# A graph layer on one core: spares' slots by one shifted row, two running extremes in bf16, places loaded one by one

## The chip, the cores and the metric

The kernel runs on one core of a Trainium2 chip. The metric is the device time of one execution in microseconds (us). The core's engines run side by side and wait for each other through semaphores: TensorE (PE, with its weight loads as PEld), VectorE (DVE), ScalarE (ACT), GpSimd (POOL) and SyncE (SP). A q behind a name (DVEq) is the engine's sequencer, which hands the instructions on in their order and does register work itself.

## The reference

400,000 edges, sorted by their destination, join 12,500 nodes of 128 features. Each edge carries the row of its source, through one of two weight matrices by the edge's type; the messages of a destination are summed; a self product, relu, a residual and a layer norm follow.

```python
msg = jnp.where((edge_types == 0)[:, None], Xs @ W_data.T + b_data, Xs @ W_control.T + b_control)
agg = jax.ops.segment_sum(msg, dst, num_segments=X.shape[0])
out = jax.nn.relu(agg + (X @ W_self.T + b_self))
x = _layernorm(x + out, axis=-1)
```

The kernel sums source rows for each destination and type first and multiplies by the weights once for each destination.

## The kernel before

Rows of x are split into three bf16 parts whose sum is the fp32 value; a row is 3 x 128 numbers. The edges come in 25 groups (`NG`) of 125 chunks of 128 edges. A group's chunks are cut into windows: "p" chunks fetch their rows from DRAM by an indirect DMA of GpSimd (985 of them, `fetch`), "e" chunks, 20 to a set, take them out of SBUF by products with 0/1 matrices on TensorE (`pick` in `picked`, L929). There are 107 sets, numbered `w`, and each is prepared two or three turns ahead.

**A set's slots.** Each of the 128 lanes holds 20 edges of a set; an edge gets a cell (which block of x its source lies in) and a rank in that cell (`block_matrix`, `ranks`, `rank_matrix`, `put`). A cell has room for 32 edges. Those of a higher rank are spares: at most `TOP` = 7 in a lane and at most `OVF` = 64 in a set. Spares of two sets, an even one and the next odd one, are placed together, so this happens 54 times (53 pairs and one set alone): `over` finds each lane's spares and packs them as `bits`; `over_before` has TensorE count the spares of the lanes before (`both["before"]`, one column for each set, in PSUM); `over_matrix` (L558) has DVE compare a table with that count; `turn` (L562) has TensorE multiply the 0/1 result with the bits; `keep` (L573 to L579) has ACT copy the outcome out and make row numbers of it, from which GpSimd fetches the spares' rows (L904).

The table `slot_col` (L368) holds o - j for spare j and slot o, 7 x 64 numbers, and the result `om_all` is 7 x 2 x 64, so that each of 7 products has the slots of both sets as its 128 columns, and 6 columns of bits stream through.

**Ranges.** `prep(g)` (L473) turns a group's edges into codes: `rel` is the destination relative to the window's start, for p and for e. Four instructions (L499) keep, in fp32, the running maximum and minimum of `rel` less its bound. At the end `check_all` makes one flag of these and other checks, and a long path would run if it were set.

**Places.** Each window's sums are added to the group's rows of sums at a place that depends on the data. `place_of` (L802) loads a group's ten places into DVE registers by one instruction, at the group's first use (25 loads), and the range check on the chip is skipped because the values were limited before. `accumulate` (L813) forms the address in the sequencer and adds (232 adds of sums `acc` and 125 of counts `cnt`).

The program order comes from `merged`, which sorts units by hand-written positions inside a turn, and from a scheduler that orders each engine's instructions.

Of the kernel before, what the change touches and what calls it, by code (L numbers as in the profile page):

```python
# [8 lines left out]
FP = mybir.dt.float32  # L9
# [10 lines left out]
P = 128  # L20
# [186 lines left out]
def short_path(ctx, tc, const, ident, eps, wT, brow, bad, x, src, dst, etype, ws, bs, out):  # L207
# [156 lines left out]
    blks = [keep.tile([P, NE, 2 * EC], BF, name=f"blk{k}") for k in range(3)]  # L364
    for t in blks:
        nc.vector.memset(t, -1.0)
    slot_col = keep.tile([P, TOP, OVF], BF, name="slot_col")
    nc.vector.tensor_copy(slot_col, iota([TOP, OVF], [[-1, TOP], [1, OVF]], 0, 0, "i5"))  # L368

    om_all = [keep.tile([P, TOP, 2, OVF], BF, name=f"om_all{k}") for k in range(2)]  # L370
    for t in om_all:
        nc.vector.memset(t, 0.0)

# [9 lines left out]
    nc.vector.memset(one_col, 0.0)  # L383
    nc.vector.memset(one_col[:, 0:PARTS], 1.0)

    worst = keep.tile([P, 5, P], FP, name="worst")
    nc.vector.memset(worst, 0.0)
    over_n = keep.tile([P, len(each_e)], BF, name="over_n")

    bounds_of, from_of, pick_first = row_tables(nc, keep, tmp)  # L390
# [10 lines left out]
    def places_and_weights():  # L401
        place = tmp.tile([1, 2, NG, NWIN], FP, name="place")
        ref = tmp.tile([1, NG, NE, 2], I32, name="ref")
        nc.gpsimd.iota(ref, pattern=[[GN, NG], [0, NE], [-PAD, 2]], base=PAD - M0, channel_multiplier=0)
        ref = ref.rearrange("o g e k -> o g (e k)")
        for at, k in enumerate("pe"):
                each = place[:, 0].rearrange("o g (i k) -> o g i k", k=2)[:, :, :, at]
                nc.vector.tensor_tensor(
                    each, first_i[k], ref.rearrange("o g (i k) -> o g i k", k=2)[:, :, :, at], op=OP.subtract
                )  # L410
        nc.vector.tensor_tensor(place[:, 1], place[:, 0], least, op=OP.max)
        nc.vector.tensor_scalar(place[:, 1], place[:, 1], float(R - WMAX), None, op0=OP.min)
        place_i = raw["place"] = keep.tile([1, NG, NWIN], I32, name="place_i")
        nc.vector.tensor_copy(place_i, place[:, 1])
        nc.vector.tensor_tensor(place[:, 0], place[:, 0], place[:, 1], op=OP.not_equal)
        nc.vector.tensor_reduce(worst[0:1, 4, 0:1], place[:, 0].rearrange("o g w -> o (g w)"), AX.X, OP.max)

        later = tmp.tile([P, 2], FP, name="later")
        for k in range(PARTS - 1):
            nc.vector.tensor_reduce(later[:, k:k + 1], ident[:, k + 1::PARTS], AX.X, OP.add)  # L420
        nc.vector.tensor_scalar(later, later, -1.0, None, op0=OP.mult)
        nc.vector.tensor_tensor(later[:, 0:1], later[:, 0:1], later[:, 1:2], op=OP.add)
        for k in range(PARTS - 1):
            nc.vector.tensor_copy(bias_b, bias)
            nc.vector.scalar_tensor_tensor(bias, bias_b, later[:, k:k + 1], bias, op0=OP.mult, op1=OP.add)
        nc.vector.tensor_copy(bias_b, bias)
        nc.vector.tensor_copy(bias, bias_b)

        wps = side()
        for i in range(3):  # L430
            nc.tensor.transpose(wps[:, i * D:(i + 1) * D], wn[:, i, :], ident)
        nc.scalar.copy(wT, wps[:, :3 * D].rearrange("p (i d) -> p i d", d=D))
# [40 lines left out]
    def prep(g):  # L473

        s, d, t = raw.pop(g)
        v = 0 if sets(g) == NE else 1
        width, high, low = (bounds_of[:GC, v, k:k + 1] for k in range(3))
        sf = pre.tile([GC, P], FP, name="sf", bufs=1)
        rel = pre.tile([GC, 2, P], FP, name="rel", bufs=1)
        code = pre.tile([GC, 2, P], FP, name="code_r", bufs=1)  # L480
        kind = pre.tile([GC, P], FP, name="kind_r", bufs=1)
        idx = pre.tile([P, GC], I32, name="idx_g", bufs=3)
# [6 lines left out]
        def rows():  # L489
            near = near_of(g, d)  # L490
            for k in range(2):
                nc.vector.tensor_scalar(rel[:, k], d, near[k], None, op0=OP.subtract)
            nc.vector.tensor_single_scalar(kind, t, 0.0, op=OP.not_equal)
            nc.vector.scalar_tensor_tensor(code[:, 1], kind, width, rel[:, 1], op0=OP.mult, op1=OP.add)
            nc.vector.scalar_tensor_tensor(code[:, 0], kind, float(PW), rel[:, 0], op0=OP.mult, op1=OP.add)
            for k, (most, least) in enumerate(((float(PW - 1), 0.0), (high, low))):
                for j, (end, op) in enumerate(((most, OP.max), (least, OP.min))):
                    w = worst[:GC, 2 * k + j, :]
                    nc.vector.scalar_tensor_tensor(w, rel[:, k], end, w, op0=OP.subtract, op1=op)  # L499

        def turn():
            ps = side()
# [40 lines left out]
    def spare_slots(w, at):  # L543

        n = w % 2 + 1
        both = joint[w // 2]
        om = om_all[w // 2 % 2]
        col = 500

        def over_before():  # L550
            both["before"] = at["rk"][:, 508:508 + n]
            nc.tensor.matmul(
                both["before"], ltri[:, 0, :], over_n[:, w + 1 - n:w + 1], start=True, stop=True, skip_group_check=True
            )

        def over_matrix():
            for k in range(n):
                nc.vector.tensor_scalar(om[:, :, k, :], slot_col, both["before"][:, k:k + 1], None, op0=OP.is_equal)  # L558

        def turn():  # L560
            for j in range(TOP):
                nc.tensor.matmul(  # L562
                    at["rk"][:, col:col + 3 * n], om[:, j].rearrange("p k o -> p (k o)"), both["bits"][:, :, :n, j],
                    start=(j == 0), stop=(j == TOP - 1), skip_group_check=True,
                )

        def keep():
            got = at["rk"][:, col:col + 3 * n].rearrange("p (v k) -> p k v", k=n)
            part = two.tile([P, 2], FP, name="part")
            for k in range(n):  # L570
                half = slice(k * OVF, k * OVF + OVF)
                code = slots[w + 1 - n + k]["code"][half, NQ - 1:NQ]
                nc.scalar.copy(  # L573
                    code, got[half, k, 2:3].rearrange("p (n o) -> p n o", o=1).to_broadcast(list(code.shape))
                )
                nc.scalar.copy(part[half], got[half, k, :2])
            idx = slots[w + 1 - n]["idx"] = two.tile([P, 1], I32, name="idx")
            rows = n * OVF
            nc.scalar.activation(idx[:rows], part[:rows, 0:1], AF.Identity, bias=part[:rows, 1:2], scale=128.0)  # L579

        return [over_before, over_matrix, turn, keep]
# [160 lines left out]
        return [(0.6, lambda: half(0, NCELL))]  # L742


    acc, added, parts_in, at_places = {}, [], {}, {}

    def sums():
        return ps2.tile([P, 512], FP, name="sums")
# [53 lines left out]
    def place_of(g, i):  # L802

        parts_in[g] = parts_in.get(g, 0) + 1
        if g not in at_places:
            with tc.issue_after(added[-2].ins) if len(added) > 1 else ExitStack():
                _, at_places[g] = nc.values_load_multi_w_load_instructions(
                    raw["place"][0:1, g, :], engines=[nc.vector.engine], min_val=0, max_val=R - WMAX,
                    skip_runtime_bounds_check_because="places are held to this range by a max and a min on the chip",
                )  # L810
        return at_places[g][i]

    def accumulate(at, rows, ps, wide, width):  # L813

# [286 lines left out]

    def check_all():

        far = keep.tile([P, 8], FP, name="far")
        nc.vector.tensor_reduce(far[:, :5], worst, AX.X, OP.max)
        for k in (1, 3):
            nc.vector.tensor_reduce(far[:, k:k + 1], worst[:, k], AX.X, OP.min)
            nc.vector.tensor_single_scalar(far[:, k:k + 1], far[:, k:k + 1], -1.0, op=OP.mult)
        nc.vector.tensor_reduce(far[:, 5:6], over_n, AX.X, OP.max)
        nc.vector.tensor_scalar(far[:, 5:6], far[:, 5:6], float(TOP), None, op0=OP.subtract)  # L1110
        pf = side()
        nc.tensor.matmul(pf[:, :pairs], one_col, over_n, start=True, stop=True)
        nc.vector.tensor_reduce(far[:, 6:7], pf[:, :pairs], AX.X, OP.max)
        nc.vector.tensor_scalar(far[:, 6:7], far[:, 6:7], float(OVF), None, op0=OP.subtract)
        nc.vector.tensor_reduce(far[:, 7:8], over_c, AX.X, OP.max)
        nc.vector.tensor_single_scalar(far, far, 0.0, op=OP.is_gt)
        nc.tensor.transpose(pf[:8, 128:128 + P], far, ident)
        most4 = keep.tile([8, 1], FP, name="most4")
        nc.vector.tensor_reduce(most4, pf[:8, 128:128 + P], AX.X, OP.max)
        nc.tensor.transpose(pf[:1, 256:264], most4, ident[:8, :8])  # L1120
        one_i = keep.tile([1, 1], FP, name="one_i")
        nc.vector.tensor_reduce(one_i, pf[:1, 256:264], AX.X, OP.max)
        nc.vector.tensor_copy(bad, one_i)

    def begin_slots(w):
# [235 lines left out]
```

## Time and profile before

| what | us |
|---|---|
| median of 3 runs | 1736.52 (1736.14 to 1736.97) |
| the profiled execution's own time | 1736.11 |
| its span, first to last instruction | 1734.3 |
| granted TensorE clock, mean | 0.992 |

| engine | busy us | share |
|---|---|---|
| ACT | 1246.5 | 72% |
| POOL | 1292.2 | 75% |

The rows of a view by line read: line, engine, operation, what is written <- what is read, shapes, count | busy time in all, mean ns of one | idle time of that engine just before, and what ended it. Rows of the chain of waits read: start, length, engine and line. A row of a wait reads: who <- for whom: us in all, how often, the longest.

### The profile page before, as it was taken

Reading aid. Unit: us, or ns where it says so; the run is one execution under the profiler, and the core shown is the slowest. Engines: PE = TensorE matmul, PEld = TensorE weight load, DVE = VectorE, ACT = ScalarE, POOL = GpSimd, SP = SyncE. Lnnn points to the kernel's source line nnn. Section 1 sums busy time; section 2 is a strip of 40 time slices with the busy share of each in tenths; the row PEclk is TensorE's granted clock in tenths of the full one; section 3 lists DMA queues with packets and bytes.
Section 4 is the critical chain, followed back from the end, with each engine's and each line's share of the span. In section 5 each row is a group of like instructions: output and inputs, shape, how many; then the busy total and the mean of one; then the engine's idle time right before and its main releaser. Section 6 shows DMA issues by size and latency. Waiting matters only on the chain.

```text
span 1734.3 us, 67322 instructions
## 1 busy us (share of the span) xinstructions
PE 1569.6 (91%) x28154; PEld 1229.6 (71%) x28154; DVE 1550.3 (89%) x3677; ACT 1246.5 (72%) x2251; POOL 1292.2 (75%) x1061
## 2 busy tenths in 40 slices
PE   0599998999899999999999999999999999999997
PEld 0376777777677777777777777777777777777776
DVE  7898999899798898998998998999998998998983
ACT  5777777677677676777776777776777776777675
POOL 0277888888878788778777787787788787778771
PEclk9999999999999999999999999999999999999999
DMA  7844454444454544454545454445444445444441
GB/s 202 293 130 128 126 154 123 141 151 130 124 157 126 157 136 141 138 157 130 156 131 150 139 150 134 147 117 170 143 148 137 144 137 154 138 145 132 125 126 57
DMA packets 148966, 248.22 MB, mean 143 GB/s; under 512 B 35937, under 2 KB 115260, under 8 KB 148652
## 3 DMA queue, kind: packets, MB, share of 16 engines
q1 hardware_dynamic: 85994, 134.45, 23.4%
q0 software_dynamic: 50032, 102.98, 22.3%
q10 hardware_dynamic: 12626, 6.40, 1.4%
q8 instruction: 222, 3.64, 0.9%
q14 instruction: 92, 0.75, 0.1%
HBM read 226.24 MB, written 17.50 MB: 141 GB/s over the span
## 4 chain that ended last, share of the span: by engine, by line
PE 41%; DVE 39%; ACT 8%; issue 6%; DMA 4%; DVEq 1%; POOL 0%; SPq 0%; ACTq 0%; POOLq 0%
PE sums L755 18%; PE got L929 13%; DVE esel L533 5%; DVE prod L639 4%; ACT emsg L943 4%; PE side L1048 4%; DVE prod L634 3%; DVE pick L741 3%; DVE rv L674 3%; DVE found L641 3%; DVE prod L612 2%; PE side L622 2%; PE side L686 2%; DVE O L533 2%; ACT h L1078 2%
## 5 line engine op out<-in xcount | busy, mean ns | idle before, releaser
L828 POOL DMA_INDIRECT msg<-rows,idx_g x985 | 1222.6, 1241 | 320.4 <-issue 147.2
L943 ACT CAST emsg<-got 128x768 bf16<-128x768 f32 (+1 forms) x1070 | 949.3, 930 | 320.3 <-PE got L929 300.1
L755 PE MATMUL sums<-esel,emsg 128*128 128x176 bf16 x7704 | 693.1, 240 | 3.9 <-DVE acc L817 3.4
L755 PEld LDWEIGHTS <-emsg 128*128 128x128 bf16 x7704 | 566.7, 98 | 117.0 <-issue 108.2
L929 PE MATMUL got<-x,pick 128*32 128x384 bf16 x10486 | 572.9, 330 | 27.7 <-DVE pick L741 13.3
L929 PEld LDWEIGHTS <-pick 128*32 128x32 bf16 x10486 | 242.5, 96 | 155.4 <-issue 24.9
L533 DVE TENSOR_TENSOR esel<-code_col,code 128x1760 bf16<-128x1760 bf16 x321 | 292.1, 910 | 14.5 <-PE sums L755 12.7
L755 PE MATMUL sums<-psel,msg 128*128 128x48 bf16 x2955 | 167.7, 184 | 14.7 <-DVE acc L817 13.0
L755 PEld LDWEIGHTS <-msg 128*128 128x128 bf16 x2955 | 138.8, 97 | 26.8 <-issue 23.7
L639 DVE TENSOR_TENSOR prod<-prod 128x1200 bf16<-128x1200 bf16 x214 | 133.7, 625 | 4.8
L634 DVE TENSOR_TENSOR prod<-O,ahead 128x2000 bf16<-128x2000 bf16 x107 | 128.4, 1200 | 2.5
L533 DVE TENSOR_TENSOR O<-cell_col,blk 128x2000 bf16<-128x2000 bf16 x107 | 127.4, 1191 | 0.9 <-ACT blk L437 0.7
L741 DVE TENSOR_SCALAR pick<-pick,lane_f 128x3200 bf16<-128x3200 bf16 x107 | 113.2, 1058 | 0.8 <-DMA pick<-there 0.8
L817 DVE TENSOR_TENSOR acc<-acc,sums 128x176 f32 (+2 forms) x232 | 66.2, 285 | 52.5 <-PE sums L755 42.2
L904 POOL DMA_INDIRECT both<-rows,idx x54 | 64.2, 1189 | 54.6 <-ACT emsg L943 28.5
L686 PE MATMUL side<-rv,O 128*128 128x64 bf16 x2140 | 83.3, 195 | 21.9 <-DVE rv L674 19.6
L533 DVE TENSOR_TENSOR psel<-near_col,near 128x1200 bf16<-128x1200 bf16 x125 | 95.8, 767 | 0.1
L686 PEld LDWEIGHTS <-O 128*128 128x128 bf16 x2140 | 79.0, 100 | 23.6 <-DVE rv L674 19.8
L674 DVE TENSOR_TENSOR rv<-rm,vals 128x1280 bf16<-128x1280 bf16 x107 | 87.7, 820 | 0.0
L641 DVE TENSOR_REDUCE found<-prod 128x20 f32<-128x600 bf16 x107 | 82.8, 774 | 2.6
L612 DVE TENSOR_TENSOR prod<-O 128x1000 bf16<-128x1000 bf16 x107 | 71.9, 672 | 0.0
L622 PEld LDWEIGHTS <-ltri 128*128 128x128 bf16 x1284 | 41.1, 96 | 38.1 <-issue 36.0
(192 smaller groups left out, 1566.8 us busy)
## 6 DMA issues: line engine op xcount, KB each, us to landing
pick<-there SPq DMA_DIRECT2D x106, 800.0 KB
msg<-rows,idx_g POOLq DMA_INDIRECT x985
acc<-acc_start SPq DMA_DIRECT2D x23, 640.0 KB
rows<-x SPq DMA_DIRECT2D x6, 1344.0 KB
xs<-in_x_dram SPq DMA_DIRECT2D x99, 62.5 KB
out_dram<-h SPq DMA_DIRECT2D x99, 62.5 KB
xt<-in_x_dram ACTq DMA_DIRECT2D x6, 896.0 KB
cnt<-cnt_start SPq DMA_DIRECT2D x22, 160.0 KB
```

The source lines that it names most:

```text
L533: nc.vector.tensor_tensor(sel.rearrange("p n (w t) -> p n w t", t=2), col[:rows].rearrange("p (o w t) -> p o w t", o=1, t=2).to_broadcast( ...
L612: nc.vector.tensor_add(h[:, :2 * CQ], s["O"][:, :2 * CQ], s["O"][:, 2 * CQ:])
L634: nc.vector.tensor_tensor(prod[:, :, :NCELL], s["O"], ahead.rearrange("p (o j) -> p o j", o=1).to_broadcast([P, EC, NCELL]), op=OP.mult,)
L639: nc.vector.tensor_add(prod[:, :, :h], prod[:, :, :h], prod[:, :, h:2 * h])
L641: nc.vector.tensor_reduce(found, prod[:, :, :h], AX.X, OP.add)
L674: placed[:] = [nc.vector.tensor_tensor(rv.rearrange("p c v (r t) -> p c v r t", t=2), rm.rearrange("p c (o r t) -> p c o r t", o=1, t=2).t ...
L686: nc.tensor.matmul(s["rk"][:m, :2 * CAP], s["held"][:, c * NCELL:c * NCELL + m], s["rv"][:, c].rearrange("p v r -> p (v r)"), start=(c == ...
L741: nc.vector.tensor_scalar(t, t, lane_f, None, op0=OP.is_equal)
L755: last = nc.tensor.matmul(out, msg[:, j * D:(j + 1) * D], sel, start=(start and j == 0), stop=stop, skip_group_check=True)
L828: return nc.gpsimd.indirect_dma_start(out=msg, out_offset=None, in_=rows3[:, :], in_offset=bass.IndirectOffsetOnAxis(ap=codes["p", g][0][: ...
L929: last = nc.tensor.matmul(ps[CAP * a:CAP * (a + 1), :], slots[w]["pick"][:, a * NQ + q, :], x3[:, 4 * q + a - a0].rearrange("p j d -> p (j ...
L943: s["out"] = nc.scalar.copy(msg[:, :n], ps[:, :n, :3 * D])
```

## The change

Three edits, and what follows from them.

1. **Slots.** The table becomes one row of 70 numbers, from -6 to 63. A set is compared once with these 70 (before: 448). For spare j the product takes 128 columns of the result, starting at column 6 - j, so the shift is made by where the weights begin. The two sets no longer share a product: each pair issues 14 products of 3 columns of bits (before: 7 of 6). One copy fetches the row numbers of both sets (before: one for each set).
2. **Ranges.** `rel` and the running extremes are bf16; one maximum and one minimum over both kinds, and the bounds are taken off at the end.
3. **Places.** One load for each window's place, 232 in all, each with a range check in DVE's sequencer.

```diff
-    slot_col = keep.tile([P, TOP, OVF], BF, name="slot_col")
-    nc.vector.tensor_copy(slot_col, iota([TOP, OVF], [[-1, TOP], [1, OVF]], 0, 0, "i5"))
-    om_all = [keep.tile([P, TOP, 2, OVF], BF, name=f"om_all{k}") for k in range(2)]
+    slot_col = table(OVF + TOP - 1, 1 - TOP, "slot_col")
+    om_all = [keep.tile([P, 2, P + TOP - 1], BF, name=f"om_all{k}") for k in range(2)]
...
-    worst = keep.tile([P, 5, P], FP, name="worst")
-    nc.vector.memset(worst, 0.0)
+    worst = keep.tile([P, 2, 2, 2, P], BF, name="worst")
+    for j in range(2):
+        nc.vector.memset(worst[:, :, j], float(j))
+    far = keep.tile([P, 12], FP, name="far")
+    nc.vector.memset(far, 0.0)
...
-        rel = pre.tile([GC, 2, P], FP, name="rel", bufs=1)
+        rel = pre.tile([GC, 2, P], BF, name="rel", bufs=1)
...
-            for k, (most, least) in enumerate(((float(PW - 1), 0.0), (high, low))):
-                for j, (end, op) in enumerate(((most, OP.max), (least, OP.min))):
-                    w = worst[:GC, 2 * k + j, :]
-                    nc.vector.scalar_tensor_tensor(w, rel[:, k], end, w, op0=OP.subtract, op1=op)
+            for j, op in enumerate((OP.max, OP.min)):
+                nc.vector.tensor_tensor(worst[:GC, v, j], worst[:GC, v, j], rel, op=op)
...
-                nc.vector.tensor_scalar(om[:, :, k, :], slot_col, both["before"][:, k:k + 1], None, op0=OP.is_equal)
+                nc.vector.tensor_scalar(om[:, k, k * OVF:k * OVF + OVF + TOP - 1], slot_col, both["before"][:, k:k + 1], None, op0=OP.is_equal)
 
         def turn():
-            for j in range(TOP):
+            for j in range(n * TOP):
+                k, j = divmod(j, TOP)
+                first = TOP - 1 - j
                 nc.tensor.matmul(
-                    at["rk"][:, col:col + 3 * n], om[:, j].rearrange("p k o -> p (k o)"), both["bits"][:, :, :n, j],
-                    start=(j == 0), stop=(j == TOP - 1), skip_group_check=True,
+                    at["rk"][:, col:col + 3], om[:, k, first:first + P], both["bits"][:, :, k, j],
+                    start=(k + j == 0), stop=(k == n - 1 and j == TOP - 1), skip_group_check=True,
                 )
...
+            nc.scalar.copy(part[:n * OVF], got[:n * OVF, :2])
             for k in range(n):
...
-                nc.scalar.copy(part[half], got[half, k, :2])
...
-        if g not in at_places:
-            with tc.issue_after(added[-2].ins) if len(added) > 1 else ExitStack():
-                _, at_places[g] = nc.values_load_multi_w_load_instructions(
-                    raw["place"][0:1, g, :], engines=[nc.vector.engine], min_val=0, max_val=R - WMAX,
-                    skip_runtime_bounds_check_because="places are held to this range by a max and a min on the chip",
-                )
-        return at_places[g][i]
+        with tc.issue_after(added[-2].ins) if len(added) > 1 else ExitStack():
+            return nc.vector.value_load(raw["place"][0:1, g, i:i + 1], min_val=0, max_val=R - WMAX)
```

`check_all` follows, with twelve columns of flags in place of eight; it runs once.

How the change moves instructions on DVE, at two places. The first is where the comparisons for the 27th pair of sets stand (`om_all<-slot_col,side`, two in a row), with the load of places near them (TENSOR_LOAD; ISA is register work of the sequencer: the address of an add, or the range check behind a load). Before, the group's ten places are loaded just behind the comparisons, and the add to `acc` behind needs the register:

```order
L666 TENSOR_SCALAR bits<-top_i 128x16
L515 SCALAR_TENSOR_TENSOR pk<-idx_g,vals_18991 128x125
L558 TENSOR_SCALAR om_all_193<-slot_col,side 128x7x64 x2
L807 TENSOR_LOAD place_i
L817 ISA
L817 TENSOR_TENSOR acc<-acc,sums 128x2x88
```

With the change:

```order
L533 TENSOR_TENSOR esel<-code_col,code 128x1760
L1071 SCALAR_TENSOR_TENSOR nm<-mv,rs 125x4
L808 TENSOR_LOAD place_i
L808 ISA x2
L533 TENSOR_TENSOR O<-cell_col_144,blk_20248 128x2000
L558 TENSOR_SCALAR om_all_194<-slot_col,side 128x70 x2
L814 ISA
L814 TENSOR_TENSOR acc<-acc,sums 128x2x88
```

A load of one place, with its two register instructions, now stands ahead of the select `O` and the comparisons; the add has no load right before it.

The second place is a little later on DVE, where a set's ranks are made into its rank matrix (`rank`, `rm`, `key`, `rv`). Before:

```order
L643 CAST rank<-found 128x40
L533 TENSOR_TENSOR rm<-rank_col,rank 128x640
L647 SCALAR_TENSOR_TENSOR key<-rank,pk 128x20
L674 TENSOR_TENSOR rv<-rm,vals_17402 128x1280
L612 TENSOR_TENSOR prod<-O 128x10x100
```

With the change:

```order
L645 CAST rank<-found 128x40
L808 TENSOR_LOAD place_i
L808 ISA x2
L533 TENSOR_TENSOR rm<-rank_col,rank 128x640
L649 SCALAR_TENSOR_TENSOR key<-rank,pk 128x20
L808 TENSOR_LOAD place_i
L808 ISA x2
L533 TENSOR_TENSOR psel<-near_col,near_19784 128x1200
L676 TENSOR_TENSOR rv<-rm,vals_19783 128x1280
```

Two loads stand inside a run of short instructions that had none.

More of the change, by code (lines that the diff above doesn't have):

```diff
@@ L415, in places_and_weights @@
         nc.vector.tensor_tensor(place[:, 0], place[:, 0], place[:, 1], op=OP.not_equal)
-        nc.vector.tensor_reduce(worst[0:1, 4, 0:1], place[:, 0].rearrange("o g w -> o (g w)"), AX.X, OP.max)
+        nc.vector.tensor_reduce(far[0:1, 8:9], place[:, 0].rearrange("o g w -> o (g w)"), AX.X, OP.max)
         later = tmp.tile([P, 2], FP, name="later")
@@ L476, in prep @@
         v = 0 if sets(g) == NE else 1
-        width, high, low = (bounds_of[:GC, v, k:k + 1] for k in range(3))
+        width = bounds_of[:GC, v, 0:1]
         sf = pre.tile([GC, P], FP, name="sf", bufs=1)
-        rel = pre.tile([GC, 2, P], FP, name="rel", bufs=1)
+        rel = pre.tile([GC, 2, P], BF, name="rel", bufs=1)
         code = pre.tile([GC, 2, P], FP, name="code_r", bufs=1)
@@ L557, in over_matrix @@
             for k in range(n):
-                nc.vector.tensor_scalar(om[:, :, k, :], slot_col, both["before"][:, k:k + 1], None, op0=OP.is_equal)
+                nc.vector.tensor_scalar(om[:, k, k * OVF:k * OVF + OVF + TOP - 1], slot_col, both["before"][:, k:k + 1], None, op0=OP.is_equal)
         def turn():
-            for j in range(TOP):
+            for j in range(n * TOP):
+                k, j = divmod(j, TOP)
+                first = TOP - 1 - j
                 nc.tensor.matmul(
-                    at["rk"][:, col:col + 3 * n], om[:, j].rearrange("p k o -> p (k o)"), both["bits"][:, :, :n, j],
-                    start=(j == 0), stop=(j == TOP - 1), skip_group_check=True,
+                    at["rk"][:, col:col + 3], om[:, k, first:first + P], both["bits"][:, :, k, j],
+                    start=(k + j == 0), stop=(k == n - 1 and j == TOP - 1), skip_group_check=True,
                 )
         def keep():
-            got = at["rk"][:, col:col + 3 * n].rearrange("p (v k) -> p k v", k=n)
+            got = at["rk"][:, col:col + 3]
             part = two.tile([P, 2], FP, name="part")
+            nc.scalar.copy(part[:n * OVF], got[:n * OVF, :2])
             for k in range(n):
@@ L573, in keep @@
                 nc.scalar.copy(
-                    code, got[half, k, 2:3].rearrange("p (n o) -> p n o", o=1).to_broadcast(list(code.shape))
+                    code, got[half, 2:3].rearrange("p (n o) -> p n o", o=1).to_broadcast(list(code.shape))
                 )
-                nc.scalar.copy(part[half], got[half, k, :2])
             idx = slots[w + 1 - n]["idx"] = two.tile([P, 1], I32, name="idx")
@@ L742, in pick_matrix @@
         return [(0.6, lambda: half(0, NCELL))]
-    acc, added, parts_in, at_places = {}, [], {}, {}
+    acc, added, parts_in = {}, [], {}
     def sums():
@@ L1102, in check_all @@
     def check_all():
[L1104 to L1110, printed above, removed]
+        most, least = (far[:, 4 * j:4 * j + 4].rearrange("p (v k) -> p v k", k=2) for j in range(2))
@@ new lines, in check_all @@
+        nc.vector.tensor_reduce(most, worst[:, :, 0], AX.X, OP.max)
+        nc.vector.tensor_reduce(least, worst[:, :, 1], AX.X, OP.min)
+        nc.vector.tensor_single_scalar(most[:, :, 0], most[:, :, 0], float(PW - 1), op=OP.subtract)
+        nc.vector.tensor_tensor(most[:, :, 1], most[:, :, 1], bounds_of[:, :, 1], op=OP.subtract)
+        nc.vector.tensor_tensor(least[:, :, 1], least[:, :, 1], bounds_of[:, :, 2], op=OP.subtract)
+        nc.vector.tensor_single_scalar(far[:, 4:8], far[:, 4:8], -1.0, op=OP.mult)
@@ L1111, in check_all @@
+        nc.vector.tensor_reduce(far[:, 9:10], over_n, AX.X, OP.max)
+        nc.vector.tensor_scalar(far[:, 9:10], far[:, 9:10], float(TOP), None, op0=OP.subtract)
         pf = side()
         nc.tensor.matmul(pf[:, :pairs], one_col, over_n, start=True, stop=True)
-        nc.vector.tensor_reduce(far[:, 6:7], pf[:, :pairs], AX.X, OP.max)
-        nc.vector.tensor_scalar(far[:, 6:7], far[:, 6:7], float(OVF), None, op0=OP.subtract)
-        nc.vector.tensor_reduce(far[:, 7:8], over_c, AX.X, OP.max)
+        nc.vector.tensor_reduce(far[:, 10:11], pf[:, :pairs], AX.X, OP.max)
@@ L1116, in check_all @@
+        nc.vector.tensor_scalar(far[:, 10:11], far[:, 10:11], float(OVF), None, op0=OP.subtract)
+        nc.vector.tensor_reduce(far[:, 11:12], over_c, AX.X, OP.max)
         nc.vector.tensor_single_scalar(far, far, 0.0, op=OP.is_gt)
[L1117 to L1120, printed above, removed]
+        nc.tensor.transpose(pf[:12, 128:128 + P], far, ident)
@@ L1121, in check_all @@
+        most4 = keep.tile([12, 1], FP, name="most4")
+        nc.vector.tensor_reduce(most4, pf[:12, 128:128 + P], AX.X, OP.max)
+        nc.tensor.transpose(pf[:1, 256:268], most4, ident[:12, :12])
         one_i = keep.tile([1, 1], FP, name="one_i")
-        nc.vector.tensor_reduce(one_i, pf[:1, 256:264], AX.X, OP.max)
+        nc.vector.tensor_reduce(one_i, pf[:1, 256:268], AX.X, OP.max)
         nc.vector.tensor_copy(bad, one_i)
```

## The prediction

> **What bounds the kernel now.** I read the page first: how busy each engine is, and the shares of the chain that ended last.
>
> ```profile
> PE 1569.6 (91%) x28154; PEld 1229.6 (71%) x28154; DVE 1550.3 (89%) x3677; ACT 1246.5 (72%) x2251; POOL 1292.2 (75%) x1061
> PE 41%; DVE 39%; ACT 8%; issue 6%; DMA 4%; DVEq 1%; POOL 0%; SPq 0%; ACTq 0%; POOLq 0%
> L828 POOL DMA_INDIRECT msg<-rows,idx_g x985 | 1222.6, 1241 | 320.4 <-issue 147.2 <-PE got L929 72.5 <-PE sums L755 55.9
> ```
>
> Two engines are near full and the chain changes between them: PE holds 41% of it, DVE with its sequencer and the issue time some 46%. So a microsecond off DVE is worth about 0.46 us at the end, one onto PE about 0.41. POOL's gathers are almost without a break, yet on the chain at 0%. Then I read who waits for whom, because every edit here touches DVE.
>
> ```profile
> DVE acc L817 <- PE sums L755: 42.2, 35, 7.9
> DVE ahead L630 <- PE side L622: 31.9, 50, 2.9
> PEld L562 <- DVE om_all L558: 21.3, 32, 1.2
> ```
>
> DVE itself waits for PE some 74 us in these two rows: what stands in front of such a wait on DVE costs nothing. In the other direction PE waits 21.3 us, in 32 of 54 cases, for the comparisons that the change shortens.
>
> **The comparisons (L558).** Rows of the view by line, shapes kept apart:
>
> ```profile
> L558 DVE TENSOR_SCALAR om_all<-slot_col,side 128x448 bf16<-128x448 bf16 x107 | 43.0, 439 | 5.3 <-PE side L552 3.7 <-ACT blk L437 0.9 <-ACT emsg L943 0.2
> L189 DVE TENSOR_SCALAR bounds_of<-row 128x1 f32<-128x1 f32 x6 | 0.6, 146 | 0.0
> L469 DVE TENSOR_SCALAR near_all<-side,from_of 125x25 f32<-125x25 f32 x2 | 0.4, 242 | 0.4 <-PE side L464 0.4
> ```
>
> 439 ns for 448 elements and 146 for one give 0.66 ns an element, so 70 elements take about 146 + 46 = 0.19 us, 0.25 less than now: 107 x 0.25 = **27 us off DVE**. Bounds: 31 if 70 cost what one does, 21 if they cost what 25 elements of PSUM do (242 ns).
>
> **The ranges (L499).** The chain has a whole `prep` of four such instructions:
>
> ```profile
> 808.84 0.20 DVE worst L499
> 809.51 0.73 DVE worst L499 x3
> ```
>
> That is 0.93 us for 25 groups, 23 us. The rows below give the durations, 283 and 344 ns, so three of them (0.97) took 0.73: each starts 0.08 before the one ahead ends.
>
> ```profile
> L499 DVE SCALAR_TENSOR_TENSOR worst<-rel,bounds_of,worst 125x128 f32<-125x128 f32 x50 | 15.2, 344 | 0.0
> L499 DVE SCALAR_TENSOR_TENSOR worst<-rel,worst 125x128 f32<-125x128 f32 x50 | 14.1, 283 | 0.0
> L602 DVE TENSOR_TENSOR prod<-blk,blk 128x400 bf16<-128x400 bf16 x107 | 39.5, 369 | 0.0
> L639 DVE TENSOR_TENSOR prod<-prod 128x600 bf16<-128x600 bf16 x107 | 50.1, 468 | 2.3
> ```
>
> The new ones are plain bf16 TENSOR_TENSOR of 256 elements. From 400 (369 ns) to 600 (468) is 0.5 ns an element, so 256 take 0.30 us, net of the overlap 0.22, two of them 0.44: **12 us off DVE**. Between 23 (free) and 5 (0.36 us net each, as the 0.44 us of a comparison now). The final check runs once; its few more columns I put at nothing.
>
> **The ten-place loads that go.** One in the chain, and the row of all:
>
> ```profile
> 814.41 0.45 DVE om_all L558
> 814.85 0.36 DVEq L807
> 815.21 1.62 issue
> 817.01 0.09 DVE acc L817
> L807 DVEq TENSOR_LOAD <-place_i x25: 1064/1320/2315, 75.0 to 1660.8; - x25
> ```
>
> Here DVE stood still from the end of the comparisons, 814.85, to the add at 817.01, 2.16 us, since a load of up to 2.3 us had nothing long in front of it. The adds' own idle rows tell how often (us, times), with causes that had long been over:
>
> ```profile
>   issue: 5.0, 3
>   PE side L1036: 4.6, 2
>   PE got L929: 4.6, 3
>   PE side L622: 4.4, 2
> ```
>
> 18.6 us in 10 cases; the other 15 loads stood behind instructions that were still running. With some share in the 42.2 us put down to PE sums I take **20 us off DVE** (not less than 10, half of the rows being true waits; not over 25 x 1.3 = 33).
>
> **The 232 loads that come.** The nearest rows are the loads of one number, once, at the kernel's end, on every engine, with the same range check on SP:
>
> ```profile
> L119 SPq TENSOR_LOAD <-bad x1: 480/480/480, 1713.1 to 1713.1; - x1
> L119 POOLq TENSOR_LOAD <-bad x1: 510/510/510, 1713.1 to 1713.1; - x1
> L119 SPq FUSED_REGOPS  x1: 187/187/187, 1713.6 to 1713.6; - x1
> L119 SPq SEQ_ASSERT  x1: 33/33/33, 1713.9 to 1713.9; - x1
> L119 PEldq TENSOR_LOAD <-bad x1: 713/713/713, 1724.0 to 1724.0; - x1
> L119 DVEq TENSOR_LOAD <-bad x1: 309/309/309, 1727.6 to 1727.6; - x1
> ```
>
> On DVE one number takes 0.31 us. SP goes from 1713.1 to 1713.9 for load (0.48) and check, so the check adds about 0.37 with its gaps; 0.31 + 0.38 makes some **0.69 us of sequencer** for each, 160 us in all. A load delays DVE only by what is left when the work already handed on runs out. In the order of the change I added, for each load, the durations of the DVE instructions between it and the last one ahead that waits for DVE itself:
>
> ```profile
> L533 DVE TENSOR_TENSOR esel<-code_col,code 128x1584 bf16<-128x1584 bf16 x107 | 104.2, 974 | 0.0
> L639 DVE TENSOR_TENSOR prod<-prod 128x1200 bf16<-128x1200 bf16 x107 | 83.6, 781 | 2.5
> L643 DVE CAST rank<-found 128x40 bf16<-128x40 f32 x107 | 20.0, 187 | 2.4
> ```
>
> 39 stand behind an `esel` of 0.97 us, 15 behind a `prod` of 0.78, with like ones 109 of the 232 are covered whole. The rest stand behind short work, such as `rank` (0.19, so 0.5 shows); their uncovered rests add up to 46 us. Part of these fall where DVE would wait for PE anyway (74 us of such waits above); I take **28 us onto DVE**, between 0 (all in such waits) and 104 (loads as dear as PE's 0.71, nothing hidden).
>
> **PE and ACT.** Each pair has 7 more products, 371 in all (749 for 378). The weight loads of seven now:
>
> ```profile
> 63.12 0.25 PEld L562 LDWEIGHTS <-om_all 128*128 128x128 bf16 x7 [0.31 <-DVE om_all L558]
> L562 PEld LDWEIGHTS <-om_all 128*128 128x128 bf16 x378 | 14.1, 96 | 22.6 <-DVE om_all L558 21.3 <-issue 0.4 <-DVE pk L515 0.3
> L576 ACT COPY part<-side 64x2 f32<-64x2 f32 x107 | 16.8, 157 | 0.0
> ```
>
> Seven end in 0.25 us, one taking 0.096: (0.25 - 0.096) / 6 = 0.026 us from one to the next. So 371 x 0.026 = **10 us onto PE**, at least that. New is that weights begin at any column, odd ones too; no row has that, and the upper bound is 0.096 for each of the 749, 62 us more. I take 0.026, since the load still has 128 columns in a row. The Trainium skill (TensorE: Matmul & The Clock Gate, Weight-path perf modes) says that the fast load of weights depends on their number, 128, and on the type not being fp32, and names no start column; by it the 10 us stand. ACT loses 53 copies of 0.157, 8 us, of which its 8% of the chain leaves under 1. PE's 21.3 us of waiting for the comparisons shrinks by up to 2 x 0.25 in 32 cases, 16 us; half of it is in the DVE term already, so I take 7 us at the end.
>
> **The sum.** DVE: -27 - 12 - 20 + 28 = -31 us, times 0.46 = -14. PE +10 x 0.41 = +4. The wait -7, ACT -1. Together **-18 us**: span 1734.3 to 1716, the profiled execution's 1736.1 to 1718, and the median of runs, 1736.5, to **1718.5**, 1.0% faster.
>
> **The rivals.**
>
> *The loads eat it all (slower).* Its place is the DVE sequencer, its price the uncovered part. Without loads DVE gains 59 us. If nothing of the uncovered part hides in existing waits, the ends meet at u where 0.46 (u - 59) + 4 - 8 = 0, u = 68 us, and that is reached when load and check take 0.84 us in place of 0.69, a load of 0.46: just what SP and POOL need (0.48, 0.51). At PE's 0.71 u is 104, and the end moves by 0.46 x 45 + 4 - 8 = +17: 1753. For it: three of four engines' rows are dearer than DVE's. Against it: DVE's row is DVE's, and its ten-place loads at 1.06 us cost a tenth each. The Trainium skill (DMA: Bandwidth & Descriptors, Latency and other measured facts) gives about 600 ns as the least that a tensor_load takes. By it u would be some 88 us, and the end +9: 1746. The 0.309 us row disagrees.
>
> *Shifted weights load slowly.* At 0.096 us each PE gets 62 us, 0.41 x 62 = +25 in place of +4: 1740. For it: no aligned row can exclude it.
>
> *POOL sets the pace.* Busy and idle before of L828 add up to 1543 us, and the 54 gathers of spares come on top:
>
> ```profile
> L904 POOL DMA_INDIRECT both<-rows,idx x54 | 64.2, 1189 | 54.6 <-ACT emsg L943 28.5 <-ACT idx L579 13.3 <-issue 8.6
> L828 POOL DMA_INDIRECT msg<-rows,idx_g x985: 943/1094/5625, 74.7 to 1699.4; - x197
> ```
>
> 1662 us are all there is from 74 to the end. Were these gathers at their rate, nothing would change: 1736. Against it: the shortest take 0.943 against a mean of 1.241, since many wait for their gate on PE, and the chain has POOL at 0%.
>
> **Chances.** The forecast 0.60, loads 0.22, weights 0.08, POOL 0.10. The likeliest time is 1718.5, with 1700 to 1732 as its own range. A measurement of this kernel tells 0.2%, 3.5 us, from no change. Faster: 0.60, plus 0.07 of the others (smaller forms of each); the same 0.09; slower 0.24. At the low end all 59 us of DVE come through with loads wholly hidden and DVE worth 0.6 rather than 0.46: -35 + 4 - 8 = -39, 1697. At the high end, 1748, most of the loads' case and that of the weights lie inside.
>
> **What would show it.** In the changed profile: the comparisons at 0.15 to 0.25 us; two range instructions at 0.30; TENSOR_LOAD on DVE, 232 of about 0.31, with the range check under 0.4; 14 weight loads of `om_all` in (13 x 0.026 + 0.096) = 0.43 us; PE's wait for `om_all` under 10 us; DVE's idle time at adds and selects put down to issue, about 28 us. Wrong would make it: loads of 0.45 or more, an idle DVE behind them of over 68 us, 14 weight loads in a microsecond, or a wait of `sums` for the fetched rows.

## The result, and the profile after

| | before | with the change |
|---|---|---|
| median of the runs | 1736.14 us (5 runs, 1734.46 to 1736.97) | 1717.82 us (5 runs, 1715.79 to 1721.01) |
| ratio to before | 1 | 0.9897 (95% interval 0.9884 to 0.9911) |
| profiled execution | 1736.1 us, span 1734.3 | 1721.0 us, span 1719.3 |

The change makes the kernel 1.0% faster, and the forecast was 1718.5 us. That the total came out so near does not yet say that its terms were right; the profile and the experiments below take them one at a time. The experiments e9 to e12 ran in two series in which the kernel before itself took 2026 and 2024 us, so those four are read as ratios to it alone.

The page of the changed kernel, busy times and the shares of the chain that ended last:

```profile
PE 1568.1 (91%) x28525; PEld 1241.5 (72%) x28525; DVE 1529.0 (89%) x3630; ACT 1243.3 (72%) x2198; POOL 1286.8 (75%) x1061
DVE 40%; PE 38%; issue 8%; ACT 5%; DMA 4%; DVEq 1%; POOL 0%; SPq 0%; ACTq 0%; POOLq 0%
```

DVE lost 21 us of busy time (1550.3 before). The span lost 15, so DVE's idle time (span less busy) went from 184 to 190 us: the two engines still take turns in the chain, in about the same shares.

The changed lines, by source line (durations are shortest, median and longest in ns, then the first and last start in us):

```profile
L558 DVE TENSOR_SCALAR om_all<-slot_col,side x107: 134/245/477, 65.7 to 1677.4; 128x70 bf16<-128x70 bf16 x107
L499 DVE TENSOR_TENSOR worst<-worst,rel x50: 275/287/291, 11.1 to 1582.4; 125x256 bf16<-125x256 bf16 x50
L808 DVEq TENSOR_LOAD <-place_i x232: 296/304/1551, 45.0 to 1707.2; - x116
L808 DVEq FUSED_REGOPS  x232: 183/190/206, 46.1 to 1707.6; - x116
L808 DVEq SEQ_ASSERT  x232: 23/23/31, 46.3 to 1707.8; - x116
```

A comparison takes 0.245 us, against 0.439 before; a range instruction 0.287; a load 0.304, with 0.190 and 0.023 for the two parts of its check. By the starts of these instructions in the trace, the check ends 0.32 us after its load (median), 78 us for all 232.

The weight loads of one pair in the timeline (start, duration), and the two rows of who waits for the comparisons:

```profile
66.42 0.46 PEld L564 LDWEIGHTS <-om_all 128*128 128x128 bf16 x14 [1.00 <-DVE om_all L558]
```

```profile
  PEld L564: 10.4, 25
  PE side L564: 6.4, 21
```

Fourteen loads end in 0.46 us, so (0.46 - 0.096) / 13 = 0.028 us from one to the next, and their start columns run through odd and even ones. PE's wait for the comparisons fell from 21.3 us to 10.4.

DVE's waits in the changed kernel (total us, times, longest):

```profile
DVE acc L814 <- PE sums L757: 41.3, 36, 7.7
DVE ahead L632 <- PE side L624: 32.3, 54, 2.0
...
DVE psel L533 <- issue: 8.7, 20, 0.5
...
DVE parts L511 <- issue: 3.4, 7, 0.7
```

The waits for PE are what they were (42.2 and 31.9). New are short stops put down to issue, none longer than 1.1 us; with the smaller rows of the same view they add up to 19 us (before: 5 us). I read them as the loads that show; without the checks behind the loads (e7) they are 2 us.

### The profile page after: what moved, and what is told of

It is laid out like the page before. It is cut to its first block, busy times and chain, and to the rows that moved or that the text cites. A ratio compares the mean times of both kernels' runs of the same rounds, so it can differ in the third digit from the quotient of the medians.

```text
span 1719.3 us, 68641 instructions
## 1 busy us (share of the span) xinstructions
PE 1568.1 (91%) x28525; PEld 1241.5 (72%) x28525; DVE 1529.0 (89%) x3630; ACT 1243.3 (72%) x2198; POOL 1286.8 (75%) x1061
## 4 chain that ended last, share of the span: by engine, by line
DVE 40%; PE 38%; issue 8%; ACT 5%; DMA 4%; DVEq 1%; POOL 0%; SPq 0%; ACTq 0%; POOLq 0%
PE sums L757 16%; PE got L926 12%; DVE esel L533 5%; DVE prod L641 5%; DVE prod L636 4%; DVE rv L676 3%; DVE pick L743 3%; DVE found L643 3%; PE side L1045 3%; ACT emsg L940 2%; DVE prod L614 2%; PE side L624 2%; DMA both<-rows,idx 2%; DVE psel L533 2%; PE side L688 2%
## 5 line engine op out<-in xcount | busy, mean ns | idle before, releaser
L814 DVE TENSOR_TENSOR acc<-acc,sums 128x176 f32 (+2 forms) x232 | 66.8, 288 | 42.1 <-PE sums L757 41.3
```

## The experiments

The theory of the prediction: DVE gets shorter by the comparisons, the ranges and the ten-place loads, the single loads give some of it back, and the end moves by 0.46 of the net. The rivals: the single loads are dearer or cheaper than that; and, after e1 to e4, that the sequence of instructions which comes with them is what counts.

### One part at a time

*e1_slots* has only the part on the comparisons and the products:

```
-    nc.vector.tensor_scalar(om[:, :, k, :], slot_col, ...)
+    nc.vector.tensor_scalar(om[:, k, k * OVF:k * OVF + OVF + TOP - 1], slot_col, ...)
```

> Only the slots edit on the kernel before. Theory (the sum of the prediction): DVE -27 x 0.46 = -12, PE +4, the wait for the comparisons -7, ACT -1: about -16 us against before. Rival (PE pays for the shifted weights or the doubled products): 0 to +10 us. Rival (the scheduler's new order decides, not the terms): anything within 8 us of zero.

Measured: 1722.70 us against 1733.52, ratio 0.9938 (0.9923 to 0.9953), 11 us faster. The sign is right, the size two thirds.

*e2_ranges* has only the two extremes in bf16:

```
-    nc.vector.scalar_tensor_tensor(w, rel[:, k], end, w, op0=OP.subtract, op1=op)
+    nc.vector.tensor_tensor(worst[:GC, v, j], worst[:GC, v, j], rel, op=op)
```

> Only the ranges edit on the kernel before. Theory: 12 us off DVE x 0.46, about -5.5 us. Rival (these stand where DVE waits anyway): 0. Rival (each microsecond of DVE counts in full): -12 us.

Measured: 1730.19 us, 0.9983 (0.9968 to 0.9998), 3 us faster; between nothing and the forecast.

*e3_places* has only the single loads:

```
-    _, at_places[g] = nc.values_load_multi_w_load_instructions(raw["place"][0:1, g, :], ...)
+    return nc.vector.value_load(raw["place"][0:1, g, i:i + 1], min_val=0, max_val=R - WMAX)
```

> Only the single loads on the kernel before. Theory: the ten-place loads give back 20 us of DVE, the 232 loads cost 28: +8 x 0.46, about +4 us. Rival (loads eat it all): +10 us or more. Rival (single loads are wholly hidden): -9 us.

Measured: 1717.39 us, 0.9909 (0.9896 to 0.9922), 16 us faster. Theory and rivals all missed it: the part that was to cost 4 us brings nearly the whole gain of the change by itself.

*e4_slots_ranges* is the changed kernel with the ten-place loads put back:

```
-    return nc.vector.value_load(raw["place"][0:1, g, i:i + 1], min_val=0, max_val=R - WMAX)
+    _, at_places[g] = nc.values_load_multi_w_load_instructions(raw["place"][0:1, g, :], ...)
```

> Slots and ranges with the ten-place loads kept. Theory: -16 - 5.5, about -22 us against before, 4 us faster than the change as a whole. Rival (single loads hidden): slower than the whole change by 5 to 9 us. Rival (loads dear): 10 us or more faster than the whole change.

Measured: 1726.91 us, 0.9954 (0.9939 to 0.9970), 7 us faster, where 22 were expected. Against the change it is 9 us slower, which is the upper end of what the rival of the hidden single loads gave. So the parts do not add up: 11 and 3 are not 7, and 7 and 16 are more than the 18 of the whole. Each of these kernels also has a sequence of its own: by their traces at least 42 (e1), 148 (e2) and 176 (e4) of DVE's some 3,570 instructions, those that write or read `worst` left out, stand elsewhere than before, so these are not pure prices of the parts. (Here and below, "at least" is the fewest that must be moved to turn one sequence of instructions into the other, loads and register work left out.)

The page of e4, busy times and the chain that ended last:

```profile
PE 1573.7 (91%) x28525; PEld 1239.5 (72%) x28525; DVE 1520.6 (88%) x3630; ACT 1243.5 (72%) x2198; POOL 1296.8 (75%) x1061
PE 46%; DVE 34%; ACT 7%; issue 6%; DMA 4%; DVEq 1%; POOL 1%; SPq 0%; ACTq 0%; POOLq 0%
```

The page of e3, busy times:

```profile
PE 1561.6 (91%) x28154; PEld 1232.3 (72%) x28154; DVE 1556.2 (90%) x3677; ACT 1245.3 (72%) x2251; POOL 1285.7 (75%) x1061
```

e4 takes 30 us of work from DVE and wins 7; e3 takes none (1556 against 1550) and wins 16. Busy time on DVE is not what decides. DVE's waits in e3:

```profile
DVE acc L812 <- PE sums L755: 35.4, 34, 5.3
DVE ahead L630 <- PE side L622: 25.3, 44, 1.8
```

They were 42.2 and 31.9. With the same work to do, DVE waits 13 us less for PE in these two rows alone. Two theories remain. L: DVE no longer stands still for the 25 long loads. O: the scheduler, which plans with the loads, places other instructions elsewhere; in the two traces at least 324 of DVE's 3,677 instructions have moved. One place, where a set's ranks are found: before,

```
L639 TENSOR_TENSOR prod<-prod 128x20x30
L533 TENSOR_TENSOR esel<-code_col,code 128x1056
L641 TENSOR_REDUCE found<-prod 128x20
L643 CAST rank<-found 128x40
```

and in e3 the third `esel` stands behind `found`, and a `psel` ahead of it:

```
L639 TENSOR_TENSOR prod<-prod 128x20x30
L533 TENSOR_TENSOR psel<-near_col,near_21310 128x1200
L641 TENSOR_REDUCE found<-prod 128x20
L533 TENSOR_TENSOR esel<-code_col,code 128x1056
L643 CAST rank<-found 128x40
```

### The stall of the ten-place loads

In the trace of before, every second ten-place load takes 2.30 us and the others 1.07 (the first one 1.32): counted from the start of the table, the ten numbers (40 bytes) of the short ones start at a multiple of 16 bytes, those of the long ones 8 bytes beside one. *e5_padded_before* is the kernel before with rows of 12 numbers, of which ten are loaded, so that each starts at a multiple of 16:

```
-    place_i = raw["place"] = keep.tile([1, NG, NWIN], I32, name="place_i")
+    place_i = raw["place"] = keep.tile([1, NG, 12], I32, name="place_i")
```

> The kernel before, with each group's ten places kept in a row of 12 numbers, so that every group starts at a multiple of 16 bytes; all engines keep their order. Theory A (the ten-place loads that take 2.3 us stand at 8-byte offsets, and their stall is what the single loads saved): all 25 loads take about 1.07 us, and the time falls by 12 to 16 us, most of what the single loads alone gave (16). Theory B (the single loads won by the new order of DVE's instructions, not by the stall): the loads get short, the time falls by 0 to 7 us (15 us of DVE x 0.46).

The loads of e5, by source line:

```profile
L807 DVEq TENSOR_LOAD <-place_i x25: 1061/1067/1317, 76.4 to 1654.4; - x25
```

Twelve loads became 1.23 us shorter, 14.8 us in all, and the sequence on every engine is that of before. Measured: 1729.88 us, 0.9977 (0.9966 to 0.9989), 4 us faster. So a microsecond of this stall is worth 0.25 us at the end. All 25 loads took 41.7 us before; at that price their going could bring 10 us (17 at the end of the interval) even if the single loads cost nothing. Theory L reaches 16 only at that far end.

### What the single loads cost

*e6_double_loads*: the change with each load made twice, the first not used.

```
+    nc.vector.value_load(raw["place"][0:1, g, i:i + 1], min_val=0, max_val=R - WMAX)
```

> The changed kernel with every single load and its check made twice (464). If a load and its check cost little because they are hidden: 0 to +6 us against the change. If they cost what I put on them (28 us of DVE for 232, x 0.46): +13. If a second one finds no cover left and each 0.68 us falls on DVE: 158 us of DVE, +40 or more.

Measured: 1751.88 us, 1.0099 (1.0084 to 1.0113), some 34 us slower than the change. That alone would make a load cost 0.147 us at the end. But at least 488 of DVE's 3,630 instructions stand elsewhere than in the change, so this run mixes the price of a load with a new sequence, and no price is taken from it.

*e7_unchecked*: the change without the range check behind each load (the check is left out, the loads stay).

```
-    return nc.vector.value_load(raw["place"][0:1, g, i:i + 1], min_val=0, max_val=R - WMAX)
+    _, at = nc.values_load_multi_w_load_instructions(
+        raw["place"][0:1, g, i:i + 1], ..., skip_runtime_bounds_check_because=...)
```

> The changed kernel with the single loads but without the range check behind each (sequencer time 0.38 in place of 0.68 us; the order is the scheduler's). Theory (loads and checks cost some 28 us of DVE): 8 to 14 us faster than the change, about 1706. Rival (they are hidden): the same, 1718.

Measured: 1719.74 us, 0.9914 (0.9901 to 0.9927), the same as the change within the intervals. Here DVE's sequence is exactly that of the change, and PE's but for four products, so it is a clean reading: of the 0.63 us of sequencer for a load with its check 0.32 went, 78 us in all, and the end did not move. DVE's waits in e7, and its chain:

```profile
DVE acc L818 <- PE sums L757: 58.9, 46, 7.7
DVE ahead L632 <- PE side L624: 38.3, 56, 1.9
PE 46%; DVE 27%; ACT 7%; DMA 6%; issue 6%; POOL 2%; DVEq 0%; ACTq 0%; POOLq 0%; SPq 0%
```

The checks were not hidden on DVE: its stops at issue fell from 19 us to 2. But the two waits for PE rose from 41.3 and 32.3 by 24 us, and DVE was idle as long as with the checks (192 us for 190). What DVE no longer lost at the checks it lost waiting for PE.

### The price of PE

*e8_more_products*: the change with 28 more products a pair, 1,512 in all, whose results nobody reads.

```
+    for j in range(28):
+        nc.tensor.matmul(at["rk"][:, 200:203], om[:, 0, j % TOP:j % TOP + P], ...)
```

> The changed kernel with 28 more products of om_all a pair, into unused columns, 54 x 28 = 1512 more at 0.026 us: 39 us onto PE. By the price of the prediction (0.41): +16 us. Rival (PE bounds the kernel): +39. Rival (DVE bounds it): below +8.

Measured: 1742.71 us, 1.0052 (1.0037 to 1.0066), 25 us slower than the change. Its weight loads, added and old:

```profile
L569 PEld LDWEIGHTS <-om_all 128*128 128x128 bf16 x1512 | 44.1, 97 | 0.0
L564 PEld LDWEIGHTS <-om_all 128*128 128x128 bf16 x749 | 25.1, 97 | 12.9 <-DVE om_all L558 10.3 <-issue 0.2
```

At 0.026 us, 1,512 products are 39 us (PE's busy time grew by 35), so a microsecond of PE costs some 0.64 us at the end, more than the 0.41 of the forecast (at least 78 of DVE's 3,630 instructions moved too, so this is not quite clean).

### The sequence held

The last four runs hold every instruction other than the loads, on all five engines, in a sequence written out: an order edge from each instruction to the next in a table of numbers, marked as one without a semaphore (`NoSync`).

```
+    tc.add_manual_dep(mine[at], last.name, DependencyInfo(NoSync, DATA), reason="pin")
```

In the traces the sequences came out as meant: e9 and e11 have that of e3 on DVE, ACT, POOL and SP without exception and on PE but for a few products that start together (4 of 28,154 in e9), e10 likewise that of before, e12 that of the change; and each has as many semaphore instructions as the kernel whose sequence it has.

*e9_ten_new_order* has the ten-place loads of before in the sequence of e3.

> The kernel before with its 25 ten-place loads, but with every other instruction of PE, DVE, ACT, POOL and SP held, by an order written out, in the sequence that it has in the kernel with the single loads alone (e3_places, which was 16 us faster than before). Theory O, the gain of the single loads is the new sequence: 10 to 18 us faster than before, the 25 loads still about 1.1 to 2.3 us each. Theory L, the gain is that DVE no longer stands still at the ten-place loads: within 4 us of before, since those loads are still there.

Measured: 2008.39 us against 2026.24, ratio 0.9891 (0.9867 to 0.9915). Its loads, by source line:

```profile
L807 DVEq TENSOR_LOAD <-place_i x25: 1060/1318/2310, 83.0 to 1928.9; - x25
```

The long loads are all there, and the gain is 1.1%, about that of e3 (0.9%).

*e10_single_old_order* has the single loads in the sequence of before.

> The 232 single loads in place of the ten-place loads, with every other instruction of all engines held in the sequence that it has in the kernel before. Theory O: no gain, from 2 us faster to 8 us slower than before, since the single loads by themselves are no better than the ten-place ones. Theory L: 12 to 18 us faster than before, as in e3_places. The sum of the prediction (20 us of DVE off, 28 us on, times 0.46) says 4 us slower.

Measured against the same 2026.24 us: 2029.67 us, 1.0024 (1.0005 to 1.0044), 0.2% slower. Theory O holds and L falls there: the sequence alone brings all, the single loads alone bring nothing. The kernel before, held in its own sequence with its own loads, was not run. That the holding itself wins 1%, and that the single loads lose it again in e10, is therefore not excluded by these two runs; against it stands e3, which gains 0.9% with single loads and nothing held.

In that series the kernel before took 2026 us, and no trace of it was kept there. The weight loads for `got` in the trace of before at 1734 us, in e3, and in e9 with the sequence of e3 (busy us, mean ns, idle before them and its causes):

```profile
L929 PEld LDWEIGHTS <-pick 128*32 128x32 bf16 x10486 | 242.5, 96 | 155.4 <-issue 24.9 <-DVE pick L741 17.6
```

```profile
L924 PEld LDWEIGHTS <-pick 128*32 128x32 bf16 x10486 | 241.4, 96 | 149.0 <-issue 18.8 <-DVE pick L741 16.8
```

```profile
L929 PEld LDWEIGHTS <-pick 128*32 128x32 bf16 x10486 | 256.0, 96 | 292.7 <-issue 184.9 <-PE got L929 4.2 <-DVE pick L741 2.3
```

A load takes the same 96 ns, but PE stood 185 us at issue in place of 19 to 25. PE is not slower throughout: from the start of one product to the next the median is 76 ns between two of `sums` in e3 and in e9 alike. It stops: in e9 there are 220 intervals of over 0.4 us between starts on PE that no wait explains, 134 us in all, where e3 and before have one each. The chain of e9 shows what bounds there:

```profile
PE 64%; ACT 12%; DVE 10%; issue 8%; another core or an unknown queue 2%; DMA 2%; DVEq 1%; SPq 0%; ACTq 0%
```

With DVE at 10% a stall on DVE is worth less there than in the 1734 us runs, which favours theory O. *e11_ten_new_again* is the same kernel as e9 once more.

> The kernel of e9_ten_new_order once more, since the kernel before took 2026 us in that call (1734 in the others), with PE issuing slower throughout. If the new sequence is the gain where the kernel before takes about 1734 us too: 12 to 20 us faster than before. If it helped only where PE is the slower engine: within 4 us of before.

Measured: 2005.89 us against 2023.50, 0.9908 (0.9889 to 0.9927). The gain repeats, but so do PE's stops (215), so the run does not answer what it was for.

*e12_ten_in_change* is the change with 25 padded ten-place loads, held in the change's own sequence.

> The changed kernel with all instructions held in its own sequence, and 25 ten-place loads (rows padded to 12 numbers, so that each takes about 1.07 us) in place of its 232 single ones. It tells what the single loads themselves cost there. Priced by the doubled loads (0.147 us each at the end) it would be up to 34 us faster than the change, less some 8 for the ten-place loads: 1690 to 1700. Theory hidden: the 232 loads stand where DVE has work or waits anyway, and it is within 5 us of the change, 1713 to 1720.

Measured against the same 2023.50 us: 1988.11 us, 0.9845 (0.9823 to 0.9866). As a ratio that lies between the two expectations (0.9845 x 1736 = 1709), below the change's 0.9897, and is the best of all. Its loads, by source line:

```profile
L809 DVEq TENSOR_LOAD <-place_i x25: 1061/1064/1877, 78.6 to 1906.1; - x25
```

So the single loads are not what makes the change fast; they may cost it up to half a per cent. Since the two ratios come from different series and the chain was another one, that is not settled, and a time for this version at the usual speed of PE was not taken.

## Why the prediction was right, and where it was not

The total was right (1718.5 for 1717.8), and the signs of two of the three parts. The sum behind it was not:

| part, by the prediction's terms | forecast at the end | measured alone |
|---|---|---|
| comparisons, products, copies: -27 x 0.46 + 4 - 7 - 1 | -16 us | -11 us (e1) |
| ranges: -12 x 0.46 | -5.5 us | -3 us (e2) |
| both together | -22 us | -7 us (e4) |
| loads: (-20 + 28) x 0.46 | +4 us | -16 us (e3) |
| all | -18 us | -18 us |

That the total came out to a microsecond is luck: two errors of some 15 us cancel. The first two parts together bring 15 us less than forecast, and the loads, which were to cost 4 us, bring some 10 on top of e4.

**The step that failed** is the one on the loads, "the ten-place loads that go" and "the 232 loads that come", and the product that follows it, "-31 us, times 0.46 = -14". It costed loads as stalls in a sequence taken as given. The sequence is itself a result of the loads: at least 324 of DVE's instructions stand elsewhere in e3, and products of PE too. Held fixed, it brings 0.9 to 1.1% with the old loads (e9, e11), and the new loads bring nothing in the old sequence (e10); both where the kernel before takes 2025 us. At the usual speed the sequence was not held, and there the case is argued: e5 prices the stall of the ten-place loads at 0.25, so that their going explains some 10 us of the 16, and all of them only at the end of the interval (17). For the rest the runs show no source but the sequence; how much of the 16 it makes at the usual speed stays open. Which of the moved instructions makes the difference was not tried apart.

**The durations held.** A load with its check was forecast at 0.31 + 0.38; the load is 0.304, and the check ends 0.32 after it. The Trainium skill (DMA: Bandwidth & Descriptors, Latency and other measured facts) has about 600 ns as the least for such a load, and by it the kernel would have ended at 1746; 232 loads on DVE have a median of 304 ns, and the measurement decides. The range instructions are 0.287 for 0.30, and DVE's busy time fell by 10 us with them alone (e2, 1539.9), for 12 forecast.

**The comparisons were mis-sized**: 0.245 us, not 0.19, so the line through 146 ns for one element and 439 for 448 lies too low at 70. The bound set beside it, the 242 ns of 25 elements with an operand in `side`, was the nearer row; the comparisons too read `side`, which the row of one element does not. 107 x 0.194 = 21 us, not 27.

**The products held**: 0.028 us between weight loads with start columns odd and even, so the rival of slow shifted weights falls. The rule of the Trainium skill (TensorE: Matmul & The Clock Gate, Weight-path perf modes), by which the fast load of weights is on when their number is 128 and the type is not fp32, agrees with it. **Their price did not**: 0.64 us at the end for each on PE (e8) in place of 0.41, so the 10 us on PE cost about 6.

**The price of DVE** was taken as its share of the chain, 0.46. The removal of pure stall came to 0.25 (e5), that of the checks' stops to nothing (e7), that of 30 us of work to 7 us, 0.22, with what else moved in it (e4). The chain's share says how much of one path an engine holds. When that path gets shorter, another through PE, hardly shorter than it, takes over: the chain has PE at 46% and DVE at 34% in e4, 46% and 27% in e7, and in e7 the time on DVE turns into waits for PE.

**PE's wait for the comparisons** halved, 21.3 to 10.4 us; under 10 was forecast. **The loads that show** make 19 us of stops at issue, where 28 were forecast, and e7 shows that removing half of each load's sequencer time, and nearly all of these stops, gains nothing. The rival *the loads eat it all* falls: it needed loads of 0.46 us, and the kernel got faster. *POOL sets the pace* falls too, since the time fell with POOL's gathers unchanged.

## What to carry to other kernels

Where a scheduler orders the instructions, an edit has two effects, its own cost and the new sequence, and the second can be the larger: hold the sequence by order edges and change one thing before a gain is put down to an edit. A share of the chain is not the price of a microsecond, and here it missed both ways: 0.46 for DVE came to 0.25 or less, 0.41 for PE to 0.64. A known dose (28 more products, 12 shorter stalls) tells the price at its place. Where an engine's stops go away and its idle time stays, they have become waits for another engine: compare its waits before the gain is booked. When parts tried alone do not add up to the whole, look at the order before looking for a cost.

## What the runs showed of the hardware

- The time of a register load of ten numbers depends on where they start: 1.07 us at multiples of 16 bytes from the table's start, 2.30 us 8 bytes beside one (twelve each in the trace of before, and all but the first, 1.32, at 1.07 in e5).
- A register load of one number took 0.304 us on DVE (median of 232), and its range check ended 0.32 us later.
- 128 bf16 weights that start at an odd column load 0.028 us apart, as those that start at an even one.
- In two series the kernel took 2024 to 2026 us in place of 1734. The traces from them (e9 to e12) have 215 to 229 stops of over 0.4 us on PE that no wait explains (one in before and in e3), 130 to 140 us in all, at a granted clock of 0.961 to 0.976 (0.992 before), while DVE's largest groups of instructions took within about 1% and the weight loads of `got` exactly (96 ns) what they took before. The record has e1 to e4, at the usual speed, on the same chip as e9 and e10, so it is not a matter of the chip alone. The runs do not say why.
